# The end of a one-core graph network: flag, branch, last half group and layer 3's form

## The chip, the cores and the metric

The kernel runs as one program on one core of a Trainium2 chip. The metric is device time in microseconds (us) of one execution. The kernel before takes 2501.71 us, the median of 4 runs (2500.54 to 2502.97). The engines are named as in the profile: PE is TensorE (matrix products), DVE is VectorE, ACT is ScalarE, POOL is GpSimd, SP is SyncE, which here only issues DMAs. Each engine works through its own queue in order; semaphores tie the queues together.

## The reference

The input `x` holds 128 graphs of 64 nodes with 256 features, `adj` a 64 x 64 adjacency for each. Four layers follow each other, each in the form `x = x + layer(relu(layernorm(x)), adj)`: two masked attention layers with 8 heads, a gated recurrent layer with five steps, and a gated graph convolution. Cut to what the change touches:

```python
    # layer 1 ends in
    return out @ Wo.T + bo                      # added to x
    # layer 3
    in_degrees = jnp.sum(jnp.abs(adj), axis=-1)
    norm = ((in_degrees + 1e-06) ** (-0.5))[..., None]
    f_hom = jnp.einsum('bnd,de->bne', x, theta) * norm
    f_hom = jnp.einsum('bnm,bmd->bnd', adj, f_hom) * norm
    f_het = jnp.einsum('bnd,de->bne', x, W_h)
    gate = jax.nn.sigmoid(jnp.einsum('bnd,de->bne', x, W_t) + b_t)
    out = gate * f_hom + (1.0 - gate) * f_het
    return jax.nn.elu(out)
```

All arithmetic is in float32.

## The kernel before, in words

Two graphs make a pair (128 rows, one SBUF partition each), four pairs a group; there are 16 groups, and a group's activations `xt` are one tile of 128 x 4 x 256. A half group is two pairs; a pair within layer 3 is called a block here.

The function `network` does not emit instructions directly. Each step is handed to a planner (`Plan.add`, through `pe`, `vec`, `vec2`, `sca`, `pool` and `dma`) with an engine, an estimated cost, the tiles it reads and writes, and a place on a time axis (`key`), which comes from the strand it is written in. `Plan.run` first moves a step's key ahead of the keys of the steps that need it (`op.key = min(op.key, u.key - ...)`), then simulates the engines with the estimated costs and emits, one after the other, the step that can start first, ties decided by the key. So the order in each engine's queue, SP's among them, is the planner's, and any estimated cost or added step can move picks far from where it stands. A load is due as early as its first user.

In the steady part, group g's attention (layers 0 and 1), group g-1's recurrent steps and group g-2's layer 3 are interleaved, with a period of one group. `attend` does the attention: `scores` (tile s, L775), `weigh` (o, L843 and L851) and the output product (y, L879); the output bias `bo` is added to `xt` on POOL (L788). `gru` does the recurrent layer: `total` sums the neighbours (agg, L1034), and `product` (L994) accumulates the gates (gb, gc, nb, nc). `back` and `back_half` do layer 3.

`back_half` works on a half group: it turns the recurrent output back (hx, L1375), adds it to `xt` (L1382), normalizes (`normed`: st L571, mv L572, pw L532, rstd L533 on POOL, xn L577), transposes (lnT L547) and takes relu (hT, L552). The products with theta, W_t and W_h follow, in `plain_products` (f L1310, gate L1314: the first holds theta, the second W_t and W_h side by side) for the last group and half of the one before, else in `seven_products` (L1339). For each block then: the gate's bias `b_t` is added (on POOL, L1399, in the last group, else on DVE, L1402), Tanh of half of it on ACT (L1404), the neighbour product on PE (hom, L1406), and on DVE hom times norm less het (L1409), times (tanh + 1) (L1412), half of it plus het (L1414), which is the convolution's output o. The elu takes ACT's Relu of -o (L1420) and Exp (L1425) in the last two groups, or DVE's `min` with 0 and Exp in the others; then max(o, 0) + exp on DVE (L1427), and that less 1 plus `xt` (L1429). Each half group is stored by one DMA on SP (L1431).

At the end the kernel guards a shortcut: the main network leaves out the softmax's maximum, and a flag tells whether that was safe. It is computed on DVE early in the last group (`flag`). `gnn_stack_kernel` reads it into a register on every engine (`values_load`, L283) and runs a second, full network under `tc.If` (L284) where it is not zero; for these inputs it is zero. In the program before, the blocks stand as: the main network; a short "false" block (on SP, eight waits for the DMA queues' semaphores, then a jump); the second network, as long as the first; the end block (L1530: SP waits for all queues and engines, and the engines meet at a barrier).

Of the kernel before, what the change touches and what calls it, by code (L numbers as in the profile page):

```python
# [11 lines left out]
ALU = mybir.AluOpType  # L12
# [265 lines left out]
def gnn_stack_kernel(tc: tile.TileContext, a: dict, out: bass.AP):  # L278
    nc = tc.nc
    with tc.tile_pool(name="flag", bufs=1) as keep:  # L280
        flag = keep.tile([P, 1], mybir.dt.int32, name="flag")
        network(tc, a, out, flag)
        beyond = nc.values_load(flag[0:1, 0:1])  # L283
        with tc.If(beyond > 0, preferred_fallthrough_block=False):  # L284
            network(tc, a, out, None)


# [1 line left out]
def network(ctx: ExitStack, tc: tile.TileContext, a: dict, out: bass.AP, flag):  # L289
# [87 lines left out]
    def load_w(name, cols):  # L377
        t = new(f"w_{name}", [P, 2, cols], 1)
        dma(cols, lambda: nc.sync.dma_start(t.tile, a[name].rearrange("(c p) o -> p c o", p=P)), [], [t])
        return t  # L380

    def load_row(name):
        t = new(f"r_{name}", [P, D], 1)
        ap = a[name]
        dma(128, lambda: nc.sync.dma_start(
            t.tile, bass.AP(tensor=ap.tensor, offset=ap.offset, ap=[[0, P], [1, D]])), [], [t])
        return t

    with plan.strand(-3.0, 0.1):
# [76 lines left out]
        load_x(1)  # L466
        of_first[1] = [load_first(1, i) for i in range(3)]
        attn.append((load_w("L1_gnn_Wo", D), load_row("L1_gnn_bo")))
        w_hh = new("w_hh", [P, 3, 7, P], 1)

        def load_hh():
# [829 lines left out]
        for half in (0, 1) if g + 1 == n_groups else (1, 0):  # L1301
            back_half(g, xt, h, adjT, norm, half)

    def plain_products(hT, F, name):

        for i in range(2):
            s = slice(i * P, (i + 1) * P)
            pf, pg = bank(f"f_{name}_{i}"), bank(f"gate_{name}_{i}")
            for kc in range(2):
                pe(mm(256), lambda kc=kc, s=s, pf=pf: nc.tensor.matmul(  # L1310
                    pf[:, :D], hT[:, kc, s], w3[:, 0, 2 * kc : 2 * kc + 2, :], start=kc == 0, stop=kc == 1),
                    [hT, w3], [pf], holds=[F[i]])
            for kc in range(2):
                pe(mm(512), lambda kc=kc, s=s, pg=pg: nc.tensor.matmul(  # L1314
                    pg.tile, hT[:, kc, s], w3[:, 1:, 2 * kc : 2 * kc + 2, :], start=kc == 0, stop=kc == 1),
                    [hT, w3], [pg], holds=[F[i]])
            vec(dve(256), lambda i=i, pf=pf: nc.vector.tensor_copy(F[i][:, 0, :], pf[:, :D]), [pf], [(F[i], 0)])
            sca(act(512), lambda i=i, pg=pg: nc.scalar.activation(
                F[i][:, 1:, :], pg.tile.rearrange("p (k d) -> p k d", k=2), AF.Copy), [pg], [(F[i], 1)])

    def seven_products(hT, F, name):

# [45 lines left out]
    def back_half(g, xt, h, adjT, norm, half):  # L1368
        ps = bank(f"hx_{g}_{half}")

        def turn():
            for i in range(2):
                for c in range(2):
                    t0 = (2 * half + i) * P
                    nc.tensor.transpose(ps[:, i * D + c * P : i * D + (c + 1) * P],  # L1375
                                        h[:, c, t0 : t0 + P], ident.tile)

        pe(437, turn, [(h, (0, half)), (h, (1, half)), ident], [ps], mode=TURN)
        for i in range(2):
            p = 2 * half + i  # L1380
            t = g * PAIRS + p
            vec(dve(256, 1), lambda i=i, t=t, p=p: nc.vector.scalar_tensor_tensor(  # L1382
                xt[:, p, :], ps[:, i * D : (i + 1) * D], cols[:, 18 + t : 19 + t], xt[:, p, :],
                op0=ALU.mult, op1=ALU.add), [ps, cols, (xt, p)], [(xt, p)])
        hT = normed(xt, half, f"{g}_3_{half}")

        F = [new("F" if g + 2 < n_groups or half else "h" if g + 2 == n_groups else ("kexp", "qk")[i], [P, 3, D], 2, f"F_{g}_{2 * half + i}") for i in range(2)]
        if g + 1 == n_groups or g + 2 == n_groups and not half:
            plain_products(hT, F, f"{g}_{half}")
        else:  # L1390
            seven_products(hT, F, f"{g}_{half}")
        for p in range(2 * half, 2 * half + 2):
            nm = f"{g}_{p}"
            v = F[p % 2]
            o = new("o", [P, D], 2, f"o3_{nm}")
            ph = bank(f"hom_{nm}")
            f, gt, het = (lambda k=k, v=v: v[:, k, :] for k in range(3))
            if g + 1 == n_groups:
                pool(650, lambda gt=gt: nc.gpsimd.tensor_tensor(gt(), gt(), b_t.tile, op=ALU.add),  # L1399
                     [(v, 0), (v, 1), b_t], [(v, "gt")])  # L1400
            else:
                vec2(dve(256), lambda gt=gt: nc.vector.tensor_tensor(gt(), gt(), b_t.tile, op=ALU.add),  # L1402
                    [(v, 0), (v, 1), b_t], [(v, "gt")])
            sca(act(256, 0.4), lambda gt=gt: nc.scalar.activation(gt(), gt(), AF.Tanh, scale=0.5),  # L1404
                [(v, "gt")], [(v, "gt")])
            pe(mm(256), lambda p=p, f=f, ph=ph: nc.tensor.matmul(  # L1406
                ph[:, :D], adjT[:, p, :], f(), start=True, stop=True), [adjT, (v, 0), (v, 1)], [ph], holds=[o])

            vec(dve(256, 1), lambda p=p, o=o, ph=ph, het=het: nc.vector.scalar_tensor_tensor(  # L1409
                o.tile, ph[:, :D], norm[:, p : p + 1], het(), op0=ALU.mult, op1=ALU.subtract),  # L1410
                [ph, norm, (v, 0), (v, 1)], [o])
            vec2(dve(256), lambda o=o, gt=gt: nc.vector.scalar_tensor_tensor(  # L1412
                o.tile, gt(), 1.0, o.tile, op0=ALU.add, op1=ALU.mult), [(v, "gt"), o], [o])
            vec2(dve(256), lambda o=o, het=het: nc.vector.scalar_tensor_tensor(  # L1414
                o.tile, o.tile, 0.5, het(), op0=ALU.mult, op1=ALU.add), [o, (v, 0), (v, 1)], [o])


            end = g + 2 >= n_groups
            if end:
                sca(act(256, 0.4), lambda o=o, gt=gt: nc.scalar.activation(gt(), o.tile, AF.Relu, scale=-1.0),  # L1420
                    [o], [(v, "gt")])
            else:
                vec2(210, lambda o=o, gt=gt: nc.vector.tensor_scalar(gt(), o.tile, 0.0, None, op0=ALU.min),
                    [o], [(v, "gt")])
            sca(act(256, 0.4), lambda gt=gt, end=end: nc.scalar.activation(  # L1425
                gt(), gt(), AF.Exp, scale=-1.0 if end else 1.0), [(v, "gt")], [(v, "gt")])
            vec2(dve(256), lambda o=o, gt=gt: nc.vector.scalar_tensor_tensor(  # L1427
                o.tile, o.tile, 0.0, gt(), op0=ALU.max, op1=ALU.add), [o, (v, "gt")], [o])
            vec2(dve(256), lambda p=p, o=o: nc.vector.scalar_tensor_tensor(  # L1429
                xt[:, p, :], o.tile, -1.0, xt[:, p, :], op0=ALU.add, op1=ALU.add), [o, (xt, p)], [(xt, p)])  # L1430
        dma(256, lambda: nc.sync.dma_start(  # L1431
            out_t[:, g * PAIRS + 2 * half : g * PAIRS + 2 * half + 2, :], xt[:, 2 * half : 2 * half + 2, :]),
            [(xt, 2 * half), (xt, 2 * half + 1)], [])

    held, chains = {}, {}
    parts = {g: front(g) for g in range(n_groups)}
    with plan.strand(FIRST, FIRST_SPAN):
# [41 lines left out]
                back(g, *held.pop(g))  # L1481
    if lean:
        with plan.strand(n_groups + 0.2, 0.1):
            once = new("once", [P, 2 * n_groups * 2 + 2], 1)
            means = slice(0, 4 * n_groups)
            vec2(200, lambda: nc.vector.tensor_scalar(
                once[:, means], sure.tile.rearrange("p n i k -> p (n i) k")[:, :, 0], 0.0, None, op0=ALU.mult),
                [sure], [once])
            n = 4 * n_groups
            vec(200, lambda: nc.vector.tensor_reduce(  # L1490
                once[:, n : n + 1], once[:, means], axis=AX.X, op=ALU.add), [once], [once])
            vec2(70, lambda: nc.vector.tensor_scalar(
                once[:, n + 1 : n + 2], once[:, n : n + 1], 0.0, None, op0=ALU.is_equal), [once], [once])
            count = bank("count")
            pe(120, lambda: nc.tensor.matmul(
                count[:1, :1], once[:, n + 1 : n + 2], few[:, parity_sum : parity_sum + 1], start=True, stop=True),
                [once, (few, 4)], [count])
            vec(70, lambda: nc.vector.tensor_scalar(
                flag[0:1, 0:1], count[:1, :1], float(P), None, op0=ALU.not_equal), [count], [])
    plan.run()  # L1500


# [31 lines left out]
```

## Time and profile before

| what | value |
|---|---|
| runs | 2501.71 us median of 4 |
| the profiled execution: its time, its span | 2501.79 us, 2499.9 us |
| mean granted TensorE clock | 0.998 |
| PE busy | 2477.0 us, 99% of the span |
| DVE, ACT, POOL busy | 1882.5, 1308.4, 895.7 us |
| DVE instructions | 4396 |
| start of the first x load on SP | 0.73 us |
| first PE product that needs x (q, L666) | 7.65 us |
| first PE product of the last half group (f, L1310) | 2480.99 us |
| issue of the last store (L1431) | 2491.50 us |

The span runs from the first instruction to the last one; the time of the execution has 1.9 us more around it. A view by line lists groups of equal instructions; the view of waits names who waited for whom; the chain of waits follows the work that ended last back to the start. A wait is put down to the semaphore that came last.

### The profile page before, as it was taken

How to read it: one execution, taken by the hardware profiler on the slowest of the kernel's cores; microseconds unless marked ns; L12 is line 12 of the kernel's file. 1: busy time of each engine (PE TensorE's matmuls, PEld its weight loads, DVE VectorE, ACT ScalarE, POOL GpSimd, SP SyncE). 2: the span in 40 equal slices, each digit the busy share in tenths (PEclk: the TensorE clock that was granted, in tenths of full speed). 3: DMA queues.
4: the chain of work that ended last, by engine and by line, in shares of the span. 5: the costliest groups of instructions: out<-in, count | busy, mean ns of one | idle time of the engine just before them, and what ended most of it. 6: DMA issues, size and time to landing. Idle time of an engine off the chain costs nothing.

```text
span 2499.9 us, 58765 instructions
## 1 busy us (share of the span) xinstructions
PE 2477.0 (99%) x24057; PEld 2130.1 (85%) x24057; DVE 1882.5 (75%) x4396; ACT 1308.4 (52%) x2654; POOL 895.7 (36%) x894
## 2 busy tenths in 40 slices
PE   9999999999999999999999999999999999999997
PEld 7788888888888888888888888888888888888885
DVE  6667777777777777787778777787777777877776
ACT  3455554555545455555555555555454555645544
POOL 5633433334233342433434233343333424332221
PEclk9999999999999999999999999999999999999999
DMA  6422212112222121212113122122211212211110
GB/s 211 158 71 86 72 54 98 64 53 84 72 80 72 62 75 66 101 52 80 59 63 102 50 96 75 53 80 72 80 68 60 77 66 80 68 50 71 52 69 19
DMA packets 78266, 188.60 MB, mean 75 GB/s; under 512 B 14802, under 2 KB 66852, under 8 KB 67108
## 3 DMA queue, kind: packets, MB, share of 16 engines
q1 hardware_dynamic: 77872, 184.71, 21.8%
q8 instruction: 192, 3.15, 0.5%
q14 instruction: 86, 0.70, 0.1%
q10 hardware_dynamic: 116, 0.04, 0.0%
HBM read 166.70 MB, written 18.02 MB: 74 GB/s over the span
## 4 chain that ended last, share of the span: by engine, by line
PE 97%; DVE 1%; ACT 0%; issue 0%; DMA 0%; POOL 0%; DVEq 0%; ACTq 0%
PE gb L994 22%; PE gc L994 17%; PE nb L994 11%; PE nc L994 8%; PE qkvb L711 6%; PE qkvc L711 5%; PE y L879 4%; PE agg L1034 3%; PE l3b L1339 3%; PE s L775 3%; PE l3c L1339 2%; PE hT L547 2%; PE lnT L547 2%; PE o L843 2%; PE o L851 1%; PE gv L930 1%
## 5 line engine op out<-in xcount | busy, mean ns | idle before, releaser
L1103 POOL TENSOR_TENSOR sn<-h,sn 128x512 f32<-128x512 f32 x158 | 202.8, 1287 | 544.7 <-ACT sn L1101 544.7
L533 POOL TENSOR_TENSOR rstd<-pw,few 128x2 f32<-128x2 f32 x128 | 96.3, 755 | 490.2 <-DVE pw L532 445.4
L994 PE MATMUL gb<-Th,w_hh 128*128 128x256 f32 x960 | 249.3, 382 | 0.0
L994 PE MATMUL gb<-Ta,gv 128*128 128x256 f32 x960 | 246.8, 380 | 0.0
L963 POOL TENSOR_TENSOR Th<-h 128x256 f32<-128x256 f32 x160 | 121.2, 777 | 299.9 <-PE nb L994 196.5
L799 POOL TENSOR_TENSOR e<-e,mask 128x512 f32<-128x512 f32 x128 | 177.4, 1406 | 111.6 <-ACT e L797 111.5
L994 PEld LDWEIGHTS gb<-Ta,gv 128*128 128x128 f32 x960 | 177.6, 190 | 22.1 <-issue 0.2
L994 PEld LDWEIGHTS gb<-Th,w_hh 128*128 128x128 f32 x960 | 175.7, 190 | 23.9 <-issue 2.4
L1101 ACT ACTIVATE sn<-sn,b_n 128x512 f32<-128x512 f32 x158 | 114.0, 722 | 144.0 <-DVE sn L1099 143.9
L1105 DVE SCALAR_TENSOR_TENSOR sn<-sg,sn 128x512 f32<-128x512 f32 x158 | 120.6, 770 | 74.3 <-POOL sn L1103 74.1
L994 PE MATMUL gc<-h,w_hh 128*128 128x256 f32 x640 | 167.7, 384 | 0.1
L994 PE MATMUL gc<-agg,gv 128*128 128x256 f32 x640 | 164.3, 379 | 0.0
L1086 ACT ACTIVATE sg<-sg,b_rz 128x512 f32<-128x512 f32 x158 | 106.5, 714 | 81.2 <-DVE sg L1066 81.2
L963 POOL TENSOR_TENSOR Th<-h,Th 128x256 f32<-128x256 f32 x160 | 144.8, 905 | 8.5 <-DVE h L1107 2.8
L552 ACT ACTIVATE hT<-lnT 128x512 f32<-128x512 f32 x96 | 57.1, 595 | 166.9 <-PE lnT L547 166.8
L994 PE MATMUL nb<-Ta,gv 128*128 128x256 f32 x480 | 144.0, 382 | 0.0
L994 PE MATMUL nb<-Th,w_hh 128*128 128x256 f32 x480 | 143.0, 380 | 0.0
L1097 DVE SCALAR_TENSOR_TENSOR sn<-sg,sn 128x512 f32<-128x512 f32 x158 | 117.8, 753 | 32.8 <-ACT sn L1208 28.3
L994 PEld LDWEIGHTS gc<-h,w_hh 128*128 128x128 f32 x640 | 116.2, 190 | 26.6 <-ACT sn L1208 4.0
L1099 DVE SCALAR_TENSOR_TENSOR sn<-sn 128x512 f32<-128x512 f32 x158 | 136.8, 872 | 2.4
L1047 DVE TENSOR_TENSOR Ta<-agg 128x256 f32<-128x256 f32 x160 | 100.3, 644 | 50.5 <-PE nb L994 27.6
L994 PEld LDWEIGHTS gc<-agg,gv 128*128 128x128 f32 x640 | 121.3, 190 | 16.7 <-issue 0.2
(228 smaller groups left out, 6565.2 us busy)
## 6 DMA issues: line engine op xcount, KB each, us to landing
gv<-gates SPq DMA_DIRECT2D x80, 1344.0 KB, 5.8
qw<-kept SPq DMA_DIRECT2D x203, 192.0 KB, 2.4
x<-in_x_dram SPq DMA_DIRECT2D x32, 256.0 KB, 2.9
out_dram<-x SPq DMA_DIRECT2D x32, 256.0 KB, 2.5
gates<-gv SPq DMA_DIRECT2D x5, 1344.0 KB, 5.7
adjq<-in_adj_dram SPq DMA_DIRECT2D x8, 256.0 KB, 4.7
gw<-in_L_gnn_weight_dram SPq DMA_DIRECT2D x5, 256.0 KB, 6.4
kept<-s SPq DMA_DIRECT2D x8, 128.0 KB, 1.8
```

What stands on the lines that cost most here:

```text
L711: nc.tensor.matmul(bk[:, j * P : (j + 1) * P], lhs, rhs, start=first and j == 0, stop=True, skip_group_check=True)
L799: pool(1225, lambda e=e: nc.gpsimd.tensor_tensor(e.tile, e.tile, bias_at(pp)[:, None, :].to_broadcast([P, 4, 2 * NODES]), op=ALU.mult), [e ...
L963: pool(690, lambda: nc.gpsimd.tensor_tensor(T[:, i, :], x(), y(), op=ALU.subtract), reads, [(T, i)])
L994: nc.tensor.matmul(bank_[:, col * HALF : (col + 1) * HALF], at(g, n), rhs(), start=first and j == 0, stop=True, skip_group_check=True)
L1047: vec2(dve(256), lambda: nc.vector.tensor_tensor(Ta[:, i, :], x(), y(), op=ALU.subtract), reads, [(Ta, i)])
L1086: sca(act(TOK, 1.5), lambda k=k, col=col: nc.scalar.activation(g_v[:, :, k, :], g_v[:, :, k, :], AF.Tanh, bias=b_rz[:, col : col + 1], sca ...
L1097: vec2(dve(TOK), lambda: nc.vector.scalar_tensor_tensor(a_(), r(), 1.0, a_(), op0=ALU.add, op1=ALU.mult), [*ts[0], n_v], [n_v])
L1099: vec2(dve(TOK), lambda: nc.vector.scalar_tensor_tensor(a_(), a_(), 0.5, b_(), op0=ALU.mult, op1=ALU.add), [n_v], [n_v])
L1101: sca(act(TOK, 1.5), lambda: nc.scalar.activation(a_(), a_(), AF.Tanh, bias=b_n[:, oc : oc + 1]), [n_v, b_n], [n_v])
L1103: pool(1230, lambda: nc.gpsimd.tensor_tensor(b_(), hh(), a_(), op=ALU.subtract), [*hp, n_v], [n_v])
L1105: vec2(dve(TOK), lambda: nc.vector.scalar_tensor_tensor(b_(), z(), 1.0, b_(), op0=ALU.add, op1=ALU.mult), [*ts[1], n_v], [n_v])
L1339: pe(mm(384), lambda: nc.tensor.matmul(bk[:, : 3 * P], b(), w3[:, :, n, :], start=first, stop=True, skip_group_check=True), [w3, *reads], ...
```

## The change

1. The branch. `network` now returns the register with the flag, loaded on all engines inside the network's own sequence (on SP ahead of the last store), and `tc.If` is told to let the second network follow the main one directly. The blocks now stand as: main network, second network, short false block, end block.
2. Layer 3's elu: `max(o, 0) + xt`, then `min(exp(o), 1)` plus that, in all groups; the `min` on DVE and the Relu on ACT go. The missing -1 is taken off layer 1's output bias row (`bo_1`), once, on DVE.
3. The last group's gate: with t = tanh(gate/2), DVE forms (t - 1) * het, ACT forms norm * t + norm, and o = 0.5 * hom * that, less 0.5 * (t - 1) * het. It is the same value as before.
4. The last half group: `plain_products` takes block 2's products, then calls all of block 2's further steps (`between`), then block 3's gate and het product ahead of its theta product. The bias `b_t` is added on DVE out of PSUM, and het copied on ACT. Each block is stored by its own DMA, and the last store comes after the flag's load on SP.

In the built program, the added step on `bo_1` is due with the first loads: its row's DMA is the first on SP, ahead of x, and the step itself is DVE's first instruction. PE has the same 12673 matmuls in another order from the 240th on; DVE has 4343 instructions that signal, 53 fewer.

```diff
-        network(tc, a, out, flag)
-        beyond = nc.values_load(flag[0:1, 0:1])
-        with tc.If(beyond > 0, preferred_fallthrough_block=False):
+        beyond = network(tc, a, out, flag)
+        with tc.If(beyond > 0, preferred_fallthrough_block=True):
             network(tc, a, out, None)
...
+        bo_1 = attn[1][1]
+        vec2(210, lambda: nc.vector.tensor_scalar(bo_1.tile, bo_1.tile, -1.0, None, op0=ALU.add), [bo_1], [bo_1])
...
+            if between:
+                vec(dve(256), lambda: nc.vector.tensor_tensor(F[i][:, 1, :], pg[:, :D], b_t.tile, op=ALU.add),
+                    [pg, b_t], [(F[i], 1)])
+                sca(act(256), lambda: nc.scalar.activation(F[i][:, 2, :], pg[:, D:], AF.Copy), [pg], [(F[i], 2)])
+                return
...
+            if between and i:
+                between()
+                others(i, s)
+                theta(i, s)
+            else:
+                theta(i, s)
+                others(i, s)
...
+            if last:
+                vec2(dve(256), lambda: nc.vector.scalar_tensor_tensor(
+                    het(), gt(), -1.0, het(), op0=ALU.add, op1=ALU.mult), [(v, "gt"), *all_of], [(v, "het")])
+                sca(act(256, 2), lambda: nc.scalar.activation(
+                    gt(), gt(), AF.Identity, scale=norm[:, p : p + 1], bias=norm[:, p : p + 1]),
+                    [(v, "gt"), (v, "het"), norm], [(v, "gt")])
+                vec(dve(256), lambda: nc.vector.scalar_tensor_tensor(
+                    o.tile, ph[:, :D], 0.5, gt(), op0=ALU.mult, op1=ALU.mult), [ph, (v, "gt")], [o])
+                vec2(dve(256), lambda: nc.vector.scalar_tensor_tensor(
+                    o.tile, het(), -0.5, o.tile, op0=ALU.mult, op1=ALU.add), [o, (v, "het")], [o])
...
-            if end:
-                sca(act(256, 0.4), lambda o=o, gt=gt: nc.scalar.activation(gt(), o.tile, AF.Relu, scale=-1.0),
-                    [o], [(v, "gt")])
-            else:
-                vec2(210, lambda o=o, gt=gt: nc.vector.tensor_scalar(gt(), o.tile, 0.0, None, op0=ALU.min),
-                    [o], [(v, "gt")])
...
+            sca(act(256, 0.4), lambda: nc.scalar.activation(gt(), o.tile, AF.Exp), [o], [(v, "gt")])
+            vec2(dve(256), lambda: nc.vector.scalar_tensor_tensor(
+                xt[:, p, :], o.tile, 0.0, xt[:, p, :], op0=ALU.max, op1=ALU.add), [o, (xt, p)], [(xt, p)])
+            vec2(dve(256), lambda: nc.vector.scalar_tensor_tensor(
+                xt[:, p, :], gt(), 1.0, xt[:, p, :], op0=ALU.min, op1=ALU.add), [(v, "gt"), (xt, p)], [(xt, p)])
...
+        if tail:
+            dma(128, lambda: nc.sync.dma_start(out_t[:, g * PAIRS + p, :], xt[:, p, :]), [(xt, p)], [])
+            ends.append((xt, p + 1))
...
+        def go():
+            if lean:
+                read.append(nc.values_load(flag[0:1, 0:1]))
+            nc.sync.dma_start(out_t[:, n_pairs - PAIRS + p, :], xt[:, p, :])
```

## The prediction, made before the changed kernel ran

> **What bounds the kernel now.** I read the page first, then the waits of TensorE by stretch, then the chain of waits of the last 35 us, then the records of the branch at the end. The page gives PE 99% busy, and its chain is 97% PE. The waits of TensorE between 152 and 2400 us, and those of the first 152 us (columns: us in total, times, longest):
>
> ```profile
> PE o L843 <- issue: 0.2, 1, 0.2
> ```
> ```profile
> PE wT L919 <- ACT e L797: 0.8, 1, 0.8
> PE q L666 <- ACT hT L552: 0.7, 1, 0.7
> PE lnT L547 <- DVE xn L577: 0.6, 2, 0.4
> PE adjT L1280 <- ACT hT L552: 0.5, 1, 0.5
> ```
>
> So in 2,248 us TensorE waits 0.2 us: whatever another engine saves there is worth nothing, and only a different matmul stream or a new wait can show. Gains are possible at the two ends alone. The chain of waits near the end (start, us, what):
>
> ```profile
> 2478.60 0.60 ACT F L1318
> ...
> 2480.45 0.49 ACT hT L552
> ...
> 2480.99 1.13 PE f L1310 x4
> ...
> 2491.05 0.42 DVE x L1429
> ```
>
> The last half group's transposed rows `hT` sat behind a Tanh on ScalarE; from its first product at 2480.99 to the last VectorE instruction it is a chain through four engines. The last store goes out at 2491.50, so 2499.9 − 2491.5 = 8.4 us lie behind it. The records of the branch (L284) and of the end block (L1530) say what they are (columns: duration min/median/max in ns, first and last start):
>
> ```profile
> L284 SPq EVENT_SEMAPHORE  x8: 17/17/17, 2494.8 to 2495.7; - x8
> L284 PEldq COMPARE_BRANCH  x2: 95/1888/3682, 2485.9 to 2487.5; - x2
> L284 ACTq COMPARE_BRANCH  x2: 38/43/48, 2490.7 to 2490.9; - x2
> L284 SPq COMPARE_BRANCH  x2: 43/46/49, 2492.5 to 2495.7; - x2
> ```
> ```profile
> L1530 SPq EVENT_SEMAPHORE  x10: 17/28/28, 2498.6 to 2499.8; - x10
> L1530 ACTq DRAIN  x2: 8/44/81, 2493.7 to 2499.4; - x2
> ```
>
> SP compares at 2492.5, falls through, and its first wait (the store's landing) ends at 2494.8, 3.3 us after the issue. Eight waits later, at 2495.74, it jumps over the fallback network, and its next instruction stands at 2498.56: 2.8 us for that jump. From there to the end are 1.34 us. ScalarE's same jump took 2490.9 to 2493.7, 2.8 us; TensorE's record of it is 3.68 us. The first branch, not taken, cost ScalarE 0.1 us.
>
> **The change, part by part.**
>
> *The branch and the flag: −2.75 us.* The fallback now follows the main block and the short "false" block stands behind it, beside the end. So the first branch is the far one, and the second goes to the next block. SP's order becomes store, branch. From the store's start: 0.37 us of issue (its row at 2491.50), 0.05 of branch and 2.82 of jump make 3.24 us; the landing beside it took 3.3 before, and I take 3.3. Then the eight waits, 0.96 (2494.79 to 2495.74), the second branch, 0.05 as recorded, and 1.34 for the end block: 5.65 instead of 8.40. With TensorE's 3.68 as the jump it would be 6.5 (−1.9); with ScalarE's 2.77 and a quicker landing of the halved store 5.6 (−2.8). If the second branch costs a whole jump too, 8.45, nothing is gained: that is a rival below. The flag's load (0.49 us, L283) moves from behind the last store to in front of it on SP. It hides in SP's wait for the last block; without that cover it would cost its 0.49. The other engines' jumps start when their work is done: VectorE's record stands at 2491.9 and ended 3.4 us later, so it is at the false block before SP needs it, with about 0.9 us to spare.
>
> [...]
>
> *The bias row first: +0.5 us.* The new subtraction of 1 from layer 1's output bias is due so early in the planner that the row's load is the first DMA on SP and the subtraction VectorE's first instruction. x's first half is then issued one issue later: 0.475 us each (0.95 for two at 0.73). Everything up to the first product (7.65) hangs on x, and TensorE runs on without slack from there to 85 us, so the 0.5 stays. Behind x wait the weights and the adjacency; they come 0.5 to 1.4 us later, with 2 us or more in hand for Wq (issued at 2.23, used at 9.78). If the row lands late, VectorE's first instruction holds up everything: in the DMA view the two output-bias rows took 5.6 us to landing under full queues, x 3.0 at the start. That bounds it: +0.3 (bandwidth alone) to +3.1 (0.73 + 5.6 + 0.42 against 3.60).
>
> *The order in the first 110 us: −1.3 us.* The new operation costs move the planner's picks from the 240th TensorE instruction on. Group 1's transposes `lnT` go in right behind `wT` at 87 instead of at 95.6, and the adjacency transposes behind group 0's first aggregation. The waits for which they stood vanish: TensorE's pitch is interrupted for 0.63 us at 96.2 (mask to adjT, 0.47 and 0.17 of it in the view) and 0.64 us at 109.4 (within lnT). The 0.8 at wT stays. Bounds: −1.6 (small stalls go as well) to 0 (new ones in their place).
>
> *The middle: 0.* The matmuls are the same 12,673. 53 VectorE instructions of some 0.34 us pitch go (56 blocks lose the `min`, a few are added), 18 us of VectorE time in all, hidden under TensorE for 2,248 us; were VectorE the bound, all 18 would show. TensorE's order changes at one place in each of eleven groups: scores before aggregation becomes aggregation before scores. I measured the changes of shape from start to start, less the pitch of the group they leave: s to agg 0.082 and agg to the following transposes 0.142, against agg to s 0.031 and s to wide 0.192. That is 0.224 against 0.223: nothing. ScalarE's Relu in the last two groups goes, behind other work.
>
> *The last group: −0.2 us.* I walk the new order with the rows' durations (VectorE 256 elements 0.42 at a pitch of 0.34, ScalarE 0.42, 0.03 to 0.04 from one engine to the next). (a) The `b_t` addition for group 14 no longer stands ahead of xn, and the Tanh at 2472.18 no longer ahead of hT: the first product f of half 0 moves from 2473.14 to 2472.45, −0.7. (b) The same products then end at 2477.9 instead of 2478.6. But on VectorE the (tanh − 1)·het of block 0 now stands ahead of the second half's rstd: it waits for the Tanh (to 2477.32), so pw moves from 2477.53 to 2478.0, rstd ends at 2478.95 instead of 2478.49, and xn at 2480.06 instead of 2479.26. On ScalarE hT stands behind Tanh, Exp and the scaled copy of block 1; that copy waits for VectorE and ends at 2481.2. hT runs 2481.1 to 2481.7, and f starts at 2481.73 instead of 2480.99: +0.74. (c) From f to the store: gate at 2.85, block 2's hom to 3.30, block 3's gate to 5.02 and its f to 5.88 (same rows as before, other order). Block 2's steps run beside them. Block 3: copy of het 5.06 to 5.44, bias added on VectorE to 5.90 (POOL's 0.72 and the waits around it gone), Tanh 6.36, multiply to 7.25, scaled copy 7.70, then the four VectorE steps 7.73, 8.24, 8.69, 9.14 to 9.56, store at 9.6. Before, it was 10.51. Sum: 0.74 − 0.91 = −0.17. Bounds: −1.0 (hT not delayed) to +0.7 (b in full, c without gain). Storing block 2 by itself costs one SP issue, 0.37, two us earlier, hidden.
>
> *Sum.* −2.75 + 0.5 − 1.3 − 0.2 = −3.75 us. The profiled execution has a span of 2499.9 in a time of 2501.79, so 2498.04; it stands 0.1 above the median 2501.71. I say **2498.0**.
>
> **The rivals.**
> 1. The second branch is not free: its place is the false block's last instruction on SP, price 2.8. Then −0.95: 2500.8. For it: no short taken jump is on record. Against: at the start SP went from one block to the next in 0.08 us (0.645 to 0.73).
> 2. More at the tail: ScalarE and VectorE get block 0 done in time, hT isn't held, f starts at 2480.3, and the small early stalls go too. −1.4 and −0.3 more: 2496.3. For it: before, POOL's addition stretched a VectorE row beside it (0.58 for 0.42 at 2487.56), which now ends. Against: the queues are in order, and the copy ahead of hT needs VectorE.
> 3. Slower: the swapped order in the eleven groups opens a wait, since scores now come 1.2 us later and ScalarE's two exponentials (1.08) with them. At 0.34 us per group it eats the 3.75; at 0.6 it gives 2504.6. Against: thirteen groups already stood so, in a stretch with 0.2 us of waits.
> 4. The early order gives nothing and the row lands late: +1.3 and +0.5, 2499.8.
>
> **How the numbers follow.** Forecast 0.55, rival 1 0.15, rival 2 0.18, rival 3 0.05, rival 4 0.07. About 0.2%, 5 us, is what a measurement can tell from no change, so the boundary lies at 2496.7 and 2506.7. Faster: rival 2 and the low edge of the forecast, 0.18. Slower by that much: rival 3 at its worst and what I missed, 0.04. The rest, 0.78, is the same. The range reaches from 2496.0 (rival 2 with the runs' scatter) to 2501.2 (rival 1 with scatter).
>
> **What would show it.** After the last store, SP's jump right behind the issue, and some 5.6 us to the end instead of 8.4. x's load issued at 1.2 instead of 0.73. No wait of adjT around 96. The first aggregation 0.8 us earlier (108.28 before). The distance from one group's aggregation to the next unchanged at 152.0. f of the last half 0.7 us later against f of the half before it plus 0.7 earlier. I am wrong if the groups' distance changes, or if SP pauses again between the false block and the end.

## The result and the profile after

The changed kernel takes 2504.58 us, the median of 40 runs (2502.16 to 2506.84). The kernel before, run beside it, takes 2501.20 us (60 runs, 2500.27 to 2503.21). The ratio is 1.0012, with a 95% interval of 1.0008 to 1.0017. That is 3.4 us more and still within the 0.2% of "no change", but it lies outside the forecast's range and on its other side.

The profiled execution took 2501.99 us with a span of 2500.2, less than any of these 40 runs; why is seen below. First, place by place, from both traces (us; the last column is what the stretch gained or lost):

| place | before | after | stretch |
|---|---|---|---|
| first product that needs x (q) | 7.65 | 9.85 | +2.20 |
| first aggregation (agg) | 108.28 | 111.98 | +1.50 |
| last aggregation | 2444.51 | 2447.38 | -0.83 |
| first f of the last group | 2473.14 | 2475.27 | -0.74 |
| first f of its second half | 2480.99 | 2485.10 | +1.98 |
| last store | 2491.50 | 2494.92 | -0.69 |
| end of the span | 2499.90 | 2500.19 | -3.14 |

*The start.* The view of TensorE's waits up to 152 us, in the changed kernel (what waited, for what, us, times, longest):

```profile
PE lnT L548 <- DVE xn L578: 2.5, 1, 2.5
...
PE wT L920 <- ACT e L798: 0.8, 1, 0.8
PE q L667 <- ACT hT L553: 0.7, 1, 0.7
```

The waits of adjT at 96 and of lnT at 109 are gone, as forecast. In their place the first lnT waits 2.5 us, because x comes late. The timeline of VectorE says what x was behind (start, us, instruction, in brackets the wait before it):

```profile
5.08 0.29 DVE L469 TENSOR_SCALAR r_L_gnn_bo<-r_L_gnn_bo 128x256 f32<-128x256 f32 x1 [5.08 <-DMA r_L_gnn_bo<-in_L_gnn_bo_dram]
5.78 0.75 DVE L572 BATCH_NORM_STATS2 st<-x 128x6 f32<-128x256 f32 x2 [0.41 <-DMA x<-in_x_dram]
```

The bias row, issued at 0.73, lands at 5.06; x's first half, issued at 1.17, lands at 5.76 (before: issued at 0.73, there by 3.57). And the wait has a second price. The view by stretches of the same run (start:end, length, then busy us of PE, PEld, DVE, ACT, POOL, the granted clock, DMA share and GB/s):

```profile
5.57:8.99 3.42, 0.94 (x6) 0.45 (x4) 2.85 (x12) 1.28 (x1) 0.74 (x2) 1.00 0.94 264
8.99:15.81 6.82, 6.13 (x18) 4.67 (x17) 3.77 (x14) 0.60 (x1) 2.54 (x4) 0.50 0.93 292
2480.24:2483.65 3.41, 1.98 (x10) 1.07 (x8) 2.82 (x9) 1.81 (x4) 1.51 (x2) 1.00 0.19 65
2483.65:2487.06 3.41, 2.17 (x9) 1.38 (x8) 2.66 (x7) 1.50 (x3) 0.00 (x0) 1.00 0.01 2
```

In the first stretch TensorE works 0.94 of 3.42 us; for the next 6.82 us its clock is granted at half, and q's first six products take 2.93 us instead of 1.56. Their rows before and after:

```profile
7.65 1.56 PE L666 MATMUL q<-hT,w_qk 128*128 128x256 f32 x6 [0.69 <-ACT hT L552]
```
```profile
9.85 2.93 PE L667 MATMUL q<-hT,w_qk 128*128 128x256 f32 x6 [0.69 <-ACT hT L553]
```

The third and fourth stretch lie in the last group, where TensorE also waits, but less, and the clock stays whole. In the profiles of several kernels below it does not.

*The last group.* The chain of waits ahead of the second half's f (start, us, what):

```profile
2481.75 0.32 DVE xn L578
2482.07 0.87 DVE o L1432
2482.94 0.33 DVE xn L578
...
2483.97 0.60 ACT F L1427
2484.57 0.49 ACT hT L553
```

Between the two xn stands a step of the other half (L1432), which takes 0.95 us beside POOL's addition (L1416) instead of 0.42, and ahead of hT stands the scaled copy (L1427), 0.60 us where 0.42 was assumed. The chain counts only the part of a step that others wait for; the timeline has its full time:

```profile
2481.86 0.80 POOL L1416 TENSOR_TENSOR F<-F,r_L_gnn_b_t 128x256 f32<-128x256 f32 x1 [0.33 <-ACT F L1326]
2481.99 0.95 DVE L1432 SCALAR_TENSOR_TENSOR o<-F,o 128x256 f32<-128x256 f32 x1
```

*The end.* The records of the branch and of the end block (duration min/median/max in ns, first and last start):

```profile
L283 SPq EVENT_SEMAPHORE  x8: 17/17/17, 2498.3 to 2498.8; - x8
...
L283 SPq COMPARE_BRANCH  x1: 45/45/45, 2495.3 to 2495.3; - x1
```
```profile
L1578 SPq EVENT_SEMAPHORE  x10: 17/28/28, 2498.9 to 2500.1; - x10
```

SP issues the last store at 2494.92, compares at 2495.33, and is in the false block at 2498.26: one jump of 2.9 us. From the eighth wait (2498.80) it goes into the end block within 0.07 us; the second branch is free. So rival 1 is out.

### The profile page after: what moved, and what is told of

Read it like the earlier page. It is cut to its first block, busy times and chain, and to the rows that moved or that the text cites. A ratio compares the mean times of both kernels' runs of the same rounds, so it can differ in the third digit from the quotient of the medians.

```text
span 2500.2 us, 58712 instructions
## 1 busy us (share of the span) xinstructions
PE 2479.6 (99%) x24057; PEld 2130.0 (85%) x24057; DVE 1847.4 (74%) x4343; ACT 1307.8 (52%) x2650; POOL 888.4 (36%) x892
## 4 chain that ended last, share of the span: by engine, by line
PE 97%; DVE 2%; ACT 0%; DMA 0%; issue 0%; POOL 0%; SPq 0%; DVEq 0%; ACTq 0%
PE gb L995 22%; PE gc L995 17%; PE nb L995 11%; PE nc L995 8%; PE qkvb L712 6%; PE qkvc L712 5%; PE y L880 4%; PE agg L1035 3%; PE l3b L1357 3%; PE s L776 2%; PE l3c L1357 2%; PE lnT L548 2%; PE hT L548 2%; PE o L844 2%; PE o L852 1%; PE gv L931 1%
## 5 line engine op out<-in xcount | busy, mean ns | idle before, releaser
L1106 DVE SCALAR_TENSOR_TENSOR sn<-sg,sn 128x512 f32<-128x512 f32 x158 | 109.0, 696 | 69.1 <-POOL sn L1104 68.9
L1098 DVE SCALAR_TENSOR_TENSOR sn<-sg,sn 128x512 f32<-128x512 f32 x158 | 117.6, 752 | 35.8 <-ACT sn L1209 29.0
L880 PE MATMUL y<-w_L_gnn_Wo,oT 128*128 128x256 f32 x512 | 133.2, 380 | 0.3 <-ACT hT L553 0.3
```

Of the source, the lines that this page charges most:

```text
L880: pe(mm(256), lambda i=i, c=c: nc.tensor.matmul(py[:, i * D : (i + 1) * D], oT[:, i, c, :], w_o[:, c, :], start=c == 0, stop=c == 1), [(oT ...
L1098: vec2(dve(TOK), lambda: nc.vector.scalar_tensor_tensor(a_(), r(), 1.0, a_(), op0=ALU.add, op1=ALU.mult), [*ts[0], n_v], [n_v])
L1106: vec2(dve(TOK), lambda: nc.vector.scalar_tensor_tensor(b_(), z(), 1.0, b_(), op0=ALU.add, op1=ALU.mult), [*ts[1], n_v], [n_v])
```

## The experiments

"late", the base of most of them, is the changed kernel with the two `bo_1` lines moved behind the loads of x, into the later strand in which layer 0's bias is prepared. That also returns TensorE to the old order of the first 110 us. All times are medians of 11 runs; the kernel before took 2501.2 to 2501.5 beside them.

### The start: four kernels

*late*

```diff
@@ strand -3.0, among the loads
-        bo_1 = attn[1][1]
-        vec2(210, lambda: nc.vector.tensor_scalar(bo_1.tile, bo_1.tile, -1.0, None, op0=ALU.add), [bo_1], [bo_1])
@@ strand -0.9
+        bo_1 = attn[1][1]
+        vec2(210, lambda: nc.vector.tensor_scalar(bo_1.tile, bo_1.tile, -1.0, None, op0=ALU.add), [bo_1], [bo_1])
```

> The changed kernel with the subtraction of 1 (and so the load of layer 1's output-bias row) moved back behind the load of x; TensorE's order of the first 110 us is that of before. Theory A (the row's load at the head of SP's queue costs the start): x issued at 0.73 again, first product q at 7.65 instead of 9.85, no stretch at half clock, first aggregation near 108.3 instead of 111.98. End -3.1, middle -1.3, last group +0.55 against before: 2501.2 - 3.85 = 2497.3. Theory B (the load costs only its issue, 0.5; the loss lies in the last group or in the middle): 2504.6 - 0.5 = 2504.1.

Measured: 2501.28 us (2498.67 to 2503.80), ratio to before 0.9998 (0.9989 to 1.0007); q at 7.97, first aggregation at 108.60, no half clock at the start. The start is repaired and 3.3 us come back, but the time is 4 us above theory A's 2497.3. Of these, 1.6 are my sum: its -1.3 for the middle is scatter (see the points below), and q is 0.3 later here. The rest, 2.4, is a second stretch at half clock. In late's view by stretches:

```profile
2478.48:2481.89 3.41, 1.48 (x7) 0.64 (x5) 2.94 (x7) 1.94 (x5) 1.36 (x2) 1.00 0.01 2
2481.89:2488.71 6.82, 6.10 (x10) 3.53 (x11) 2.55 (x6) 1.20 (x4) 0.00 (x0) 0.50 0.12 40
```

TensorE works 1.48 of 3.41 us between the halves of the last group, then runs at half clock through the second half's products: from f to the last hom 9.98 us, where the changed kernel's profiled run, at whole clock, took 7.02. TensorE's waits in late from 2468 to 2500 us (what waited, for what, us, times, longest):

```profile
PE f L1310 <- ACT hT L553: 2.0, 2, 1.2
...
PE lnT L548 <- DVE xn L578: 1.4, 2, 0.9
```

Between the halves stand 0.6 and 0.9 us for the two xn and 1.2 us for hT.

*late_one_row and late_128_rows*: one more load at the head of SP's queue, into the same tile; the planner leaves every TensorE and ScalarE instruction of late in its place. For one row:

```diff
         t = new(f"r_{name}", [P, D], 1)
         ap = a[name]
+        if name == "L1_gnn_bo":
+            plan.add("SP", 450, lambda: nc.sync.dma_start(t.tile, bass.AP(tensor=ap.tensor, offset=ap.offset, ap=[[0, P], [1, D]])), [], [t], early=8000.0)
```

For 128 rows the source is `a["L1_gnn_Wo"][:P, :]`; the row itself is loaded later in both, as in late.

> As the run late, with the row's load issued once more as the first DMA on SP (128 partitions read the same 1 KB); VectorE has no instruction that waits for it. Theory A1 (the transfer itself holds up x): x's first half lands near 5.8 instead of 3.6, q near 9.9, half clock for some 7 us, first aggregation near 113, time near 2502.3 (late + 5). Theory A2 (VectorE's subtraction at the head of its queue was the wait): x is one issue late, q near 8.1, time near 2497.8 (late + 0.5).

> As the run late_one_row, but the first DMA on SP reads 128 different rows of 1 KB (the first half of a weight) into the same tile; everything else is the same. Theory A1a (reading the same 1 KB 128 times is slow): 128 KB at the 300 to 377 GB/s that before shows at 2.5 to 4 us is 0.35 to 0.45 us, with 0.45 of issue x lands near 4.4, q near 8.4, no half clock, time near 2498.1 (late + 0.8). Theory A1b (any 128 KB ahead of x does it): as late_one_row, near 2502.3.

Measured: 2504.68 us (2502.84 to 2508.51) with one row, ratio 1.0013 (1.0004 to 1.0022); 2502.47 us (2499.00 to 2506.31) with 128 rows, ratio 1.0005 (0.9996 to 1.0014). One row costs late 3.4 us in the median (A1 expected 5), 128 rows cost 1.2 (A1a expected 0.8). The DMA view of the first 8 us, 40 equal slices, and the landing of the first load: one row,

```profile
GB/s 0 0 0 0 0 0 0 0 5 97 82 97 97 77 72 133 141 179 213 225 179 261 330 364 356 348 379 389 359 358 338 271 251 190 251 265 250 270 252 236
...
r_L_gnn_bo<-in_L_gnn_bo_dram SPq DMA_DIRECT2D x1, 128.0 KB, 4.3
```

and 128 rows:

```profile
GB/s 0 0 0 0 0 0 0 0 41 102 282 282 143 210 287 346 346 341 348 336 236 241 302 297 269 271 282 346 287 275 280 289 285 277 245 219 268 328 302 320
...
r_L_gnn_bo<-in_L_gnn_Wo_dram SPq DMA_DIRECT2D x1, 128.0 KB, 2.1
```

The same 128 KB into the same tile take 4.3 us when 128 partitions read one row, and 2.1 us when they read 128 rows; from 1.8 to 3 us the first moves 72 to 97 GB/s, the second 102 to 287, and VectorE can start on x, queued behind, at 5.69 or at 4.06. q follows at 10.08 or 8.10. VectorE has no instruction that waits for the row here, so A2 is out: it is the transfer, and its one-row source (A1a). In late_one_row q's first six products take 2.93 us, as at half clock in the changed kernel, the record of the granted clock begins, whole, at 14.24 us, and the first aggregation comes at 112.75; with 128 rows at 108.74. The 1.2 us of the medians between late and late_128_rows are more than the 0.14 of the first aggregation; both scatter by 5 us or more, and the profiles of both have the fall in the last group.

*warm30*: `for _ in range(30)` instead of 20 in the warm-up transposes.

> The changed kernel with 30 instead of 20 warm-up transposes (0.222 us each: TensorE is busy to 8.0 instead of 5.79, lnT begins at 8.27); nothing else differs. If the gap before lnT brings the half clock: granted clock 1.00 in every window of the first 20 us, q still at 9.85, first aggregation near 109.2 (2.8 earlier than 111.98: 5.0 lost at the start, counted without the early order's 1.3, less 2.2 that q is late), time near 2501.8 and less scatter. If the clock has another cause: half speed at 9 to 16 us again, 2504.6.

Measured: 2502.28 us (2499.87 to 2504.98), ratio 1.0002 (0.9993 to 1.0011). The clock is whole from 7.14 us to 2481.81, and q runs at full pace:

```profile
9.53 1.56 PE L667 MATMUL q<-hT,w_qk 128*128 128x256 f32 x6 [0.69 <-ACT hT L553]
```

The first aggregation comes at 108.77, 3.2 us earlier than in the changed kernel. Of these, 0.3 is that x landed earlier in this execution (5.46 instead of 5.76), so of the start's +3.70 the clock is 2.9; 2.3 us of the median go. What is left at the first aggregation, +0.49, is x's delay of 1.88 (q) less 1.39 for the early order, against the 1.3 forecast. The fall in the last group is in this profile too (2481.81 to 2488.63), in the changed kernel's own order.

### The last group: six kernels

*late_fill*: late, and idle transposes in TensorE's waits between the halves.

```diff
                 to = ps[:, i * P : (i + 1) * P]
+                if name == f"lnT_{n_groups - 1}_3_1":
+                    for _ in range((8, 2, 0, 0)[i]):
+                        nc.tensor.transpose(ps[:, P : 2 * P], ident.tile, ident.tile)
...
+            def product(kc):
+                for _ in range(6 if between and not i and not kc else 0):
+                    nc.tensor.transpose(pf[:, :P], ident.tile, ident.tile)
+                nc.tensor.matmul(
+                    pf[:, :D], hT[:, kc, s], w3[:, 0, 2 * kc : 2 * kc + 2, :], start=kc == 0, stop=kc == 1)
```

> The run late, with 16 idle transposes put into TensorE's waits between the two halves of the last group (8 before the first transpose of lnT, 2 behind it, 6 before the first f); every other instruction and its order is that of late. Theory C (between 2479.1 and 2482.6 us TensorE works only 0.88 of 3.53 us, and in most executions the clock falls to half for 6.83 us): granted clock 1.00 from there to the end, f to the last hom 7.4 instead of 10.4 us, span near 2497.7 and times of 2499.0 with no execution beyond about 2501; the median 2.3 under late's 2501.28. Theory D (the clock's fall is not brought by TensorE's waits, or costs nothing, since VectorE and ScalarE set the end): 2501.3 again, with the same scatter.

Measured: 2498.81 us (2498.38 to 2500.53), ratio 0.9990 (0.9981 to 0.9999). Its stretch there:

```profile
2478.11:2481.52 3.41, 2.79 (x22) 2.23 (x20) 2.94 (x7) 1.95 (x6) 1.16 (x2) 1.00 0.01 2
```

TensorE is kept at 2.79 of 3.41 us, the clock stays whole, 2.5 us of the median go and most of the scatter with them, though the second half's f still comes 9.84 us after the first's. Theory C holds; D is out. It also explains the changed kernel's profiled run: in it the fall did not come (1.98 and 2.17 us of work).

*late_form0 and after_form0*: the old form of the steps for blocks 0 and 1, in late and in the changed kernel.

```diff
-            if last:
+            if tail:
                 vec2(dve(256), lambda: nc.vector.scalar_tensor_tensor(
                     het(), gt(), -1.0, het(), op0=ALU.add, op1=ALU.mult), [(v, "gt"), *all_of], [(v, "het")])
```

> The run late, with the elementwise steps of block 0 and 1 of the last group in the form of all other groups (no (tanh - 1) * het on VectorE, no scaled copy on ScalarE); TensorE's, POOL's and SP's orders are those of late. Theory E (these steps stand ahead of the second half's rstd, xn and hT and make f to f 9.83 instead of 7.85): f to f near 7.9, no half clock, time near 2497.0 (2499.0 without the half clock, less 2.0). Theory F (the delay has another cause, POOL's additions beside VectorE): f to f near 9.8, time near 2501.3.

> The changed kernel with the same edit as late_form0 and nothing else. If the last group's delay and its half clock add to the row's cost at the start: 2504.6 - 2.0 - some 2 = 2500.6, first aggregation at 112 as in the changed kernel. If the loss lies at the start alone: 2504.6.

Measured: 2503.45 us (2502.10 to 2504.29), ratio 1.0007 (0.9998 to 1.0016), and 2506.18 us (2505.00 to 2508.01), ratio 1.0020 (1.0011 to 1.0029). Both are worse than their base; E and F both missed. From f to f it is 12.17 us in late_form0 and 12.18 in after_form0. The timeline of VectorE in late_form0 shows why:

```profile
2479.16 0.48 DVE L1435 SCALAR_TENSOR_TENSOR o<-hom,norm,F 128x256 f32<-128x256 f32 x1 [0.69 <-PE hom L1421]
2479.75 0.58 DVE L1438 SCALAR_TENSOR_TENSOR o<-F,o 128x256 f32<-128x256 f32 x1
...
2482.65 0.40 DVE L578 TENSOR_SCALAR xn<-x,mv,rstd 128x256 f32<-128x256 f32 x1
```

POOL has rstd ready at 2479.26 (its row is 0.71 from 2478.55), but nine of the first half's elementwise steps stand between pw and the first xn, which starts at 2482.65. TensorE works 0.49 of 3.41 us and falls to half clock. So the old form alone brings nothing back; what stands out is where xn stands in VectorE's queue. The profile of late_form0 also has a fall at the start, though its loads stand as in late: TensorE works 1.87 us from 4.32 to 7.73, its clock is at half to 11.14, and the first aggregation comes at 109.90 instead of 108.60. A fall at the start does not need the row.

*late_xn and late_rush*: the old order's virtue put back by due time, with the new form.

```diff
+        rush = 6000.0 if name == f"{n_groups - 1}_3_1" else 0.0
         xn = new("xn", [P, 2, D], 1, f"xn_{name}")
...
-                op0=ALU.subtract, op1=ALU.mult), [(xt, p), mv_of(i), rstd], [(xn, i)])
+                op0=ALU.subtract, op1=ALU.mult), [(xt, p), mv_of(i), rstd], [(xn, i)], rush)
@@ late_rush only
-                   f"lnT_{name}", True, writes, relu=True, by_graph=by_graph)
+                   f"lnT_{name}", True, writes, relu=True, by_graph=by_graph, early=rush)
```

> The run late with the two xn of the last half put ahead on VectorE (a lower due time in the planner); the planner moves pw, rstd and the additions of hx with them. Form of the steps unchanged. Theory G (it is the order on VectorE that makes f to f 9.83, not the form): f to f near 8.1 and TensorE's waits there too short for the half clock: time near 2497.1 (2498.8 without the half clock, less 1.7). Rival (ScalarE's scaled copy ahead of hT holds it): f to f above 9, time 2498.5 or, with the half clock, 2501.

> As late_xn, with lnT on TensorE and hT's copy on ScalarE put ahead as well: TensorE then goes from the first half's last hom straight to the second half's f. f to f by TensorE's own rows: f 0.97 + gate 1.72 + f 0.86 + lnT 0.44 + gate 1.72 + hom 0.43 = 6.2 instead of 9.83, no wait, no half clock. If from f to the last store it stays at 9.8: 2498.8 - 3.6 = 2495.2. Rival (the steps of the first half that are moved back on VectorE and ScalarE hold the second half): f to the store 11.8, time 2497.2.

Measured: late_xn 2496.41 us (2495.68 to 2498.30), ratio 0.9979 (0.9970 to 0.9988); late_rush 2496.40 us (2495.71 to 2498.64), ratio 0.9981 (0.9972 to 0.9990). Both beat both kernels. In late_xn the timeline of VectorE has

```profile
2474.63 0.73 DVE L579 TENSOR_SCALAR xn<-x,mv,rstd 128x256 f32<-128x256 f32 x2
```

both xn 4.6 us earlier than late's first (2479.18; its second at 2480.38), or 4.1 counted from each run's first f, and in one piece. From f to f it is 7.09 us, less than the 8.1 expected, and the wait ahead of f is 0.36; the clock stays whole. Theory G holds in the main, but no run moves xn alone: ScalarE's queue moved with it. Block 1's scaled copy stands ahead of hT in late and behind it in late_xn (late, then late_xn):

```profile
2481.48 0.60 ACT L1427 ACTIVATE F<-F,norm 128x256 f32<-128x256 f32 x1 [0.55 <-DVE F L1425]
2481.99 0.58 ACT L553 ACTIVATE hT<-lnT 128x512 f32<-128x512 f32 x1
```
```profile
2478.80 0.58 ACT L553 ACTIVATE hT<-lnT 128x512 f32<-128x512 f32 x1
...
2480.23 0.59 ACT L1428 ACTIVATE F<-F,norm 128x256 f32<-128x256 f32 x1
```

In late the copy can have held hT for some 0.6 us (lnT's row ends at 2481.38, hT starts at 2481.99). That is the most the rival can claim of the 2.74 us from f to f; the rest was lost ahead of it, with the second xn at 2480.38.

late_rush has the 6.1 us from f to f that were worked out, but 10.4 from there to the last store where late_xn has 9.88, so it gains nothing more: the chain is VectorE's and ScalarE's by then. A part of its rival (held by the steps moved back) is right.

*after_busy*: the changed kernel with both fillers.

> The changed kernel with both fillers of TensorE's waits (30 warm-up transposes as in warm30, 16 idle ones in the last group as in late_fill) and nothing else: what is left of the loss is then not the clock's. Theory (two separate half-clock phases, at the start and in the last group): granted clock 1.00 throughout, first aggregation near 108.8, f to the last hom 7.4, time 2499.1 (late_fill's 2498.81 plus the 0.3 of the first aggregation) with a scatter of about 2. Rival (one phase only moves to another place, or the row's delay is felt all the same): 2502 or more.

Measured: 2500.02 us (2498.71 to 2500.95), ratio 0.9992 (0.9983 to 1.0001). The fillers take 4.6 us off the changed kernel's 2504.58; warm30 alone gave 2.3 and late_fill 2.5 to late, so the two falls add up. The time is 0.9 above the theory's 2499.1, and the granted clock was not whole throughout. The profiled run has a short fall at a third place, ahead of the last group:

```profile
2435.42:2438.83 3.41, 1.84 (x8) 0.94 (x7) 3.38 (x11) 1.32 (x2) 1.96 (x2) 1.00 0.00 0
2438.83:2442.24 3.41, 3.41 (x7) 1.72 (x6) 2.83 (x8) 0.49 (x1) 2.38 (x4) 0.50 0.00 0
```

### The end: one kernel

*branch*: the kernel before, with `preferred_fallthrough_block=True` and nothing else.

> The kernel before with the fallback network behind the main block (one argument), the flag still loaded behind the last store. The jump then runs beside the store's landing: from the last store to the end 8.40 - 2.8 = 5.6, the median 2501.2 - 2.8 = 2498.4. If the second branch costs a jump as well: 2501.2.

Measured: 2499.05 us (2498.44 to 2500.55), ratio 0.9991 (0.9982 to 1.0000). Its records of the branch and the end block:

```profile
L284 SPq EVENT_SEMAPHORE  x8: 17/17/17, 2495.1 to 2495.7; - x8
...
L284 SPq COMPARE_BRANCH  x1: 45/45/45, 2492.2 to 2492.2; - x1
```

The store goes out at 2491.24, then the flag's load (0.49), the jump (2.9), and the end at 2497.08: 5.84 us instead of 8.40, so the branch is worth 2.56 in the trace and 2.1 in the medians (2.8 expected). The changed kernel has 5.26 from the last store to the end. The 0.58 between them are the flag's load, now ahead of the store (0.49 in its row), and 0.09 that no run here tells apart.

## Why the prediction was wrong, point by point

- *What failed first: "The bias row first: +0.5 us".* The step priced the row's load at one issue and kept +3.1 as its far end; measured, the load costs 2.2 us at q alone, and late to late_one_row gives +3.4 in the median. The bound for a late row was on the page (the DMA view's 5.6 us for such rows), but I read it as the price of full queues. It is the row's own: 4.3 us with nothing ahead of it in the queue. And I took VectorE's wait as the danger, while x's transfer behind the row was the loss.
- *What the sum had no term for: the clock.* Every wait was priced at its length. The 2.5 us ahead of lnT cost 2.9 more at the first aggregation (2.2 of delay at q, 2.9 of half clock and -1.4 for the order make the +3.7), and the waits of the last group 2.5 in the median. Within each of these traces the falls and rises of the granted clock lie whole multiples of 3.4133 us apart: in the changed kernel it falls at 8.99, rises at 15.81, two of them later, and falls again at 2493.89, another 726 later; in the kernel before the record begins at 6.21 and the one fall, at 2491.11, stands 728 later; in late_one_row 724 lie between 14.24 and 2485.49. Such a stretch is called a window here. Up to the last product, the windows ahead of a fall were not idle: they held from 0.49 (late_form0, in the last group) to 1.87 us (late_form0, at the start) of work. At half clock the changed kernel's window with 2.72 us of work (8.99 to 12.40) did not bring whole clock back, and the next, with 3.41, did; in after_busy the first had 3.41 (2438.83 to 2442.24) and did. So the return took 3.41 us there, and 6.82 in the changed kernel and in late. What decides a fall, no run shows. My sum gave the clock no price at either place; warm30 puts it at 2.9 us at the start, late_fill at 2.5 in the last group.
- *"The last group: -0.2 us" was mis-sized at (b).* (a) was right, -0.74 for -0.7. (b) has 9.83 - 7.85 = +1.98 from f to f instead of +1.44: I put the two xn together, and the planner put L1432 (0.95 us beside POOL) between them, and the scaled copy took 0.60 instead of 0.42. (c) gave -0.69 for -0.91. The sum is +0.55 at whole clock, near the far bound of +0.7, and about +3 with the fall.
- *"The branch and the flag: -2.75 us" was right*, -3.14 measured: the jump over the fallback (2.9 us) runs beside the store's landing, and the second branch goes on within 0.07 us. Why the one takes 2.9 and the other 0.07, no run shows. The store's landing, taken as 3.3, was no limit (2.1 us here), and the eight waits took 0.54 instead of 0.96 behind it.
- *"The order in the first 110 us: -1.3 us" was right*: both waits are gone, and warm30 and after_busy have 1.39 between their delay at q and at the first aggregation. No kernel isolates it.
- *"The middle: 0" stands.* From first to last aggregation: 2336.2 before, 2335.4 after; but branch, with before's code there, has 2335.7, and the nine other kernels with the new form and no fall of the clock there lie between 2334.9 and 2337.1. The -0.83 of the table is scatter; rival 3 did not happen.

By the changed kernel's own terms: +3.7 at the start, -0.8, +0.5, -3.1 make the +0.3 between the two profiled spans. The medians lie 3.4 apart for two more reasons: before's profiled run lay 0.6 above its median (2501.79 against 2501.20), and the changed kernel's median holds the fall in the last group, which late_fill prices at 2.5 us. The changed kernel's own profile doesn't have that fall; the profile of warm30, with the same last group, has it. With fillers against both falls the kernel takes after_busy's 2500.0.

Open: why one row is slow to read for 128 partitions (only the source was exchanged), and what decides whether half clock follows a window (1.59 us of work in branch: no; 1.62 in late_one_row: yes). The scatter of the kernel before (2500.3 to 2503.4) may be falls like after_busy's near 2435 us or late_form0's at the start, but its profile has none.

## What to carry to other kernels

Look at which DMA a planner puts first: the load that everything waits for goes out first, and a row that is spread over all partitions goes behind it, whoever needs it: ahead of x it cost 2.2 us at q here. Price a new wait of TensorE twice, by its length and by what the clock does after it: waits of 0.6, 0.9 and 1.2 us within 3.6 us cost 2.5 us of half clock here, which idle transposes or an order without the waits took away again. And in a kernel's last steps, where nothing covers them, check each in-order queue for work of the other half standing ahead of what releases TensorE; here one changed due time, with the steps that the planner moved along with it (late_xn), took 4.9 us off late.

## What the runs showed of the hardware that was not expected

- One row read by 128 partitions: 4.3 us for 128 KB with nothing ahead of it in the queue (late_one_row), against 2.1 us from 128 rows (late_128_rows).
- The granted clock by windows of 3.4133 us, up to the last product: at whole clock, windows with 0.49 and 1.87 (late_form0), 0.94 (the changed kernel), 0.96 (after_form0), 1.48 (late), 1.50 (warm30, late_128_rows), 1.62 (late_one_row) and 1.84 us of work (after_busy) were followed by half clock; 1.59 (branch), 1.87 (after_busy), 1.98 (the changed kernel) and 2.00 (the kernel before) were not. Whole clock came back behind windows with 3.41 us of work (the changed kernel, after_busy), and not behind the one with 2.72 (the changed kernel).
- Idle transposes in TensorE's waits went with whole clock: with 16 of them late_fill has 2.79 us of work in a window of the last group, where late has 1.48 and falls; with ten more in the warm-up, warm30 has 3.68 us of work from 4 to 8 us, where the changed kernel has 1.79 and falls at 8.99.
- Where the windows lie differs from one profile to the next: counted back to the start of the span, the first full one begins 2.16 us into it in the changed kernel (record from 5.57), 2.80 in the kernel before (from 6.21), 0.40 in late (fall at 2481.89) and 2.55 in late_128_rows (fall at 2480.63). late scatters by 5.1 us, late_fill by 2.2; that the place of the windows is behind this is my estimate.
- In the changed kernel an ACT step with both its scale and its bias taken from a tile (L1427) took 0.60 us for 256 elements; Tanh (L1419) and Exp (L1442) with constants took 0.42.
